# A four-layer attention kernel: the MLP in blocks of 512 pixels and two rounds, and a reordered top

## The chip, the cores and the metric

The kernel runs on one core of one Trainium2 chip, in one launch. The metric is the device time of an execution in microseconds, the median of the runs shown. A second execution under the hardware profiler gave the profile and the trace; TensorE's granted clock in it is 1.00 of full speed.

## What is computed

The input is `x`, two images of 512 channels and 32 x 32 pixels, all in float32. Four layers follow each other:

- Layer 0, deformable attention and an MLP. Queries come from a grouped 1x1 convolution. A strided depthwise convolution of the queries gives 64 offsets for each of the 8 groups of each image, at which keys and values are sampled. A small network of 2 inputs, 128 and 128 inner units and 1 output is evaluated for every pair of a pixel and a sample: `relu(relu(pos @ w1 + b1) @ w2 + b2) @ w3 + b3`. It is added to the attention logits. After softmax, values and output projection come `x = x + out` and the MLP:

```
xn2 = bn(x, bn2_g, bn2_b)
h1 = gelu(mlp_w1 @ xn2 + mlp_b1)        # 512 -> 2048 channels
x = x + mlp_w2 @ h1 + mlp_b2            # 2048 -> 512 channels
```

- Layers 1 and 2, group norm and self attention over the 1024 pixels, with 8 heads and with 1 head, and a projection with a bias.
- Layer 3, attention with 64 query and key channels and a factor `gamma`.

## The kernel before, in words

**Order of the work.** Each engine runs its instructions in the order in which the Python program emits them: `in_order` (line 61) ties each instruction to the one before it on its engine. Semaphores between engines come from what the tiles are written and read by. So a statement that moves in the program moves in the queue of every engine that it uses. DMAs are issued from the queues of SyncE, ScalarE and POOL, among the other instructions of that queue.

**The top (lines 205 to 900).** ScalarE's queue issues the loads of the query weights, of the first quarter of image 0 and of the weights of layer 2. `transposed(j, k)` transposes four 128x128 pieces of row block `k` of `qkv2` (`j`: q, k or v) on TensorE, and ScalarE copies them to SBUF. With these, `fold` multiplies layer 2's weights into each other. `bias_weights` sorts the inner units of the small network, `offsets(0)` computes the first offsets on VectorE, and `small_fold` computes two bias vectors of layer 2. The second of these is a row of 512 numbers: four matmuls `pb` (line 880), each of 32 weight columns that repeat one column of the value bias, write four groups of 32 partitions; ScalarE copies the result to `o_row`, and four DMAs spread it over the partitions. `bias_row` (line 1795) does the same for layer 1 as one of the chores between matmul groups.

**The pair loop (lines 901 to 993).** 256 steps. `first` (line 615) makes two tiles of the first inner layer on VectorE with one custom instruction, `second` (line 632) multiplies them by `cpb_w2`, four matmuls of 32 columns side by side, and ScalarE takes the relu. Sums of the results go through VectorE and accumulating DMAs. The results lie in two rings, `h2p` and `h2j`, which were slices of the tile `bridge` (8 x 4 KB per partition), and the tiles of `first` in `ring`.

**The end of the attention.** `finish_last` (line 733) runs the last softmax and projection, and between its steps forms what the MLP needs: `normed_rights` computes the normed pixels of the first block on POOL and their sums on VectorE, `left_sums` the sums of the columns of `mlp_w1`.

**The MLP (lines 1283 to 1395).** Both products use the seven-product form of a two by two block product (Strassen-Winograd): `lefts` and `rights` form sums of the four blocks of the weights and of the pixels, `products` runs seven products, and `combined` adds them up on VectorE. The pixels come in blocks of `BLK` = 256, of which each half of `PX` = 128 is one side of the block product, so matmuls have 128 moving columns. For each of 8 blocks there are 8 chunks `c` of the first product; each yields 128 lower and 128 upper inner units (2048 in all). ScalarE copies product 1 from PSUM (`first_of`), VectorE combines, ScalarE applies Gelu (`activated`), VectorE forms the sums of the right side for the second product (`form_right2`). The second product has two output chunks of 8 k-steps and ends in `added`, which adds bias and residual and stores the result to DRAM (`x_d`) for a fallback path. In PSUM the seven products of a chunk lay in two banks of 512 float32, four in each.

Between these, group norm of layer 1 advances in steps (`norm`), whose last four write the normed image `hc` with ScalarE; the sums of `mlp_w2` are formed in block 0 (`later`); in the last block the weights `qkv1` are loaded into the place of `mlp_w1`.

## Time and profile before

| | us |
|---|---|
| median of 3 runs | 3326.72 (3326.65 to 3328.97) |
| the profiled execution | 3326.56 |
| its span | 3324.8 |
| TensorE busy | 3311.0 |
| VectorE busy | 2643.8 |
| ScalarE busy | 1809.0 |
| POOL busy | 672.8 |
| first matmul of the pair loop (L632) | at 53.82 |
| first matmul of the MLP (pma) | at 1999.67 |
| first matmul of layer 1 (pm) | at 2402.69 |

The span is the time from the first to the last instruction of the program. Of each group of instructions the profile gives line, engine, operation, the tiles that it writes and reads, the shape and the count, then busy time and mean duration, then idle time before it and what ended that. L632 is line 632 of the kernel. PE is TensorE's matmuls, PEld its weight loads, which run beside them, DVE is VectorE, ACT ScalarE, SP SyncE; a q behind a name is the engine's queue, which issues DMAs. A float32 matmul call leaves two matmul records and two weight loads in the trace. The ends of matmuls are modelled and overlap the next one's start, so rates are taken from start to start.

### The profile page before, as it was taken

What the parts mean: (1) busy time and instruction counts of PE and PEld (TensorE: products, weight loads), DVE (VectorE), ACT (ScalarE), POOL (GpSimd) and SP (SyncE); (2) the same over time, 40 slices, a digit from 0 to 9 for tenths busy, and PEclk for the clock granted to TensorE, in tenths of its full rate; (3) what the DMA queues carried; (4) which work ended last, traced back from release to release, by engine and by line L of the source; (5) the groups of instructions that cost most, each with busy time, mean ns of one, the idle gap of its engine ahead of it and who ended that gap; (6) DMA issues with size and microseconds to landing.
All of it is one profiled execution on the core that took longest, in us unless ns stands there. A gap on an engine that the chain in (4) does not pass through costs nothing.

```text
span 3324.8 us, 60957 instructions
## 1 busy us (share of the span) xinstructions
PE 3311.0 (100%) x24805; PEld 1599.6 (48%) x24805; DVE 2643.8 (80%) x3027; ACT 1809.0 (54%) x2771; POOL 672.8 (20%) x804
## 2 busy tenths in 40 slices
PE   9999999999999999999999999999999999999999
PEld 4333333333333333333333339999953443687777
DVE  7999999999998799999999976455446466665656
ACT  4866877877876677877877642122126245122221
POOL 1333333333333233333333310000000000000000
PEclk9999999999999999999999999999999999999999
DMA  5787787787787577787787741000100100000111
GB/s 177 164 168 151 159 167 158 160 166 152 160 167 159 107 160 155 159 170 158 163 164 155 160 116 58 14 8 14 52 0 14 26 32 17 7 7 4 29 33 37
DMA packets 143121, 342.87 MB, mean 103 GB/s; under 512 B 37104, under 2 KB 52592, under 8 KB 142064
## 3 DMA queue, kind: packets, MB, share of 16 engines
q0 software_dynamic: 68112, 230.21, 37.1%
q1 hardware_dynamic: 71472, 102.12, 10.1%
q10 hardware_dynamic: 3248, 6.56, 0.5%
q8 instruction: 197, 3.23, 0.4%
q14 instruction: 92, 0.75, 0.1%
HBM read 71.46 MB, written 10.83 MB: 25 GB/s over the span
## 4 chain that ended last, share of the span: by engine, by line
PE 97%; issue 1%; ACT 1%; DVE 1%; POOL 0%; ACTq 0%; DVEq 0%; POOLq 0%
PE z L632 53%; PE pw L1479 6%; PE pma L135 6%; PE pmb L135 5%; PE pmv L1479 4%; PE score L1660 4%; PE pv L1672 3%; PE pm L1479 3%; PE score L1479 3%; PE pmt L1479 1%; PE ppr L1479 1%; PE pp L721 1%; PE sim L661 1%; PE pf L135 1%; PE pma L1382 1%
## 5 line engine op out<-in xcount | busy, mean ns | idle before, releaser
L632 PE MATMUL z<-wa,cpb_w 128*32 128x512 f32 x10880 | 1193.1, 593 | 0.5
L641 ACT ACTIVATE h<-z,b2h 128x1024 f32<-128x1024 f32 x768 | 851.2, 1113 | 327.7 <-PE z L632 316.9
L615 DVE CUSTOM_DVE_ANT_1 wa<-tab,pairs 128x2048 f32<-128x2048 f32 x340 | 779.3, 2293 | 2.7 <-PE z L632 2.4
L632 PEld LDWEIGHTS z<-wa,cpb_w 128*32 128x32 f32 x10880 | 346.1, 110 | 806.0 <-issue 713.5
L632 PE MATMUL z<-h,cpb_w 128*32 128x512 f32 x5504 | 609.4, 593 | 0.3 <-ACT h L641 0.2
L615 DVE CUSTOM_DVE_ANT_1 h<-tab,pairs 128x2048 f32<-128x2048 f32 x172 | 394.4, 2294 | 1.2 <-PE z L632 1.0
L632 PEld LDWEIGHTS z<-h,cpb_w 128*32 128x32 f32 x5504 | 175.4, 110 | 409.5 <-issue 360.1
L646 DVE SCALAR_TENSOR_TENSOR h<-h,turn,h 128x1024 f32<-128x1024 f32 x256 | 329.4, 1287 | 5.5 <-ACT h L641 5.5
L641 ACT ACTIVATE bridge<-z,b2h 128x1024 f32<-128x1024 f32 x162 | 180.6, 1115 | 118.2 <-PE z L632 118.2
L966 POOL DMA_DIRECT2D bridge<-bridge x150 | 127.5, 850 | 532.7 <-DMA bridge<-h 502.3
L646 DVE SCALAR_TENSOR_TENSOR bridge<-bridge,turn,h 128x1024 f32<-128x1024 f32 x162 | 208.1, 1285 | 3.0 <-ACT bridge L641 2.9
L974 POOL DMA_DIRECT2D bridge<-h x160 | 150.3, 939 | 287.3 <-DVE h L646 166.2
L1322 ACT COPY p<-pma 128x128 f32<-128x128 f32 x80 | 21.2, 266 | 335.7 <-PE pma L135 335.7
L1314 DVE TENSOR_TENSOR upper<-pma,p 128x256 f32<-128x256 f32 x80 | 33.8, 422 | 178.9 <-ACT p L1322 178.8
L1661 ACT ACTIVATE p<-score 128x512 f32<-128x512 f32 x256 | 129.7, 628 | 79.8 <-PE score L1660 79.4
L966 POOL DMA_DIRECT2D h2j<-h2j x90 | 76.2, 846 | 312.3 <-DMA h2j<-h 296.7
L1693 DVE TENSOR_TENSOR acc<-acc,p 128x1024 f32<-128x1024 f32 x96 | 111.4, 1219 | 28.4 <-ACT p L1661 28.4
L641 ACT ACTIVATE h2j<-z,b2h 128x1024 f32<-128x1024 f32 x94 | 104.9, 1116 | 42.7 <-PE z L632 42.7
L646 DVE SCALAR_TENSOR_TENSOR h2j<-h2j,turn,h 128x1024 f32<-128x1024 f32 x94 | 121.1, 1288 | 0.2
L1660 PE MATMUL score<-q,k 64*128 64x512 f32 x512 | 119.6, 604 | 0.0
L1672 PE MATMUL pv<-p,vT 128*64 128x512 f32 x512 | 116.5, 598 | 0.0
L979 POOL DMA_DIRECT2D bridge<-bridge x90 | 110.4, 1226 | 1.2 <-DMA bridge<-bridge 0.9
(468 smaller groups left out, 4363.2 us busy)
## 6 DMA issues: line engine op xcount, KB each, us to landing
bridge<-h POOLq DMA_DIRECT2D x160, 512.0 KB, 5.1
h2j<-h POOLq DMA_DIRECT2D x93, 512.0 KB, 5.5
bridge<-bridge POOLq DMA_DIRECT2D x159, 256.0 KB, 3.6
tab<-slog_d SPq DMA_DIRECT2D x128, 256.0 KB, 5.0
h2j<-h2j POOLq DMA_DIRECT2D x90, 256.0 KB, 3.3
bridge<-bridge POOLq DMA_DIRECT2D x150, 128.0 KB, 5.4
bridge<-bridge SPq DMA_DIRECT2D x90, 128.0 KB, 3.7
bridge<-h2j SPq DMA_DIRECT2D x90, 128.0 KB, 3.6
```

What stands on the lines that cost most here:

```text
L135: nc.tensor.matmul(pm, w, m, start=(k == 0), stop=(k == len(pairs) - 1))
L615: nc.vector._custom_dve(TENSOR_ADD_SAT, out=h1, in0=tx.unsqueeze(1).to_broadcast([P, H, 2, W]), in1=ty.unsqueeze(3).to_broadcast([P, H, 2, ...
L632: nc.tensor.matmul(z[point * 32 : point * 32 + 32, n], cpb_w2[:, lo : lo + 32], h1s[point][:, half * 16 : half * 16 + 16, :], start=True, ...
L641: nc.scalar.activation(h2, z, AF.Relu, bias=b2h[:, part : part + 1])
L646: nc.vector.scalar_tensor_tensor(h2, h2, turn[:, part // 2 : part // 2 + 1], parts.pop(part + 1), ALU.mult, ALU.add)
L966: nc.gpsimd.dma_start(out=own[0:P:2], in_=own[1:P:2], accum_op=ALU.add)
L974: nc.gpsimd.dma_start(out=joins[i - 1], in_=other, accum_op=ALU.add)
L1479: nc.tensor.matmul(out, stationary(l, k), moving(r, k), start=start and k == 0, stop=k == nk - 1, skip_group_check=not start,)
L1660: nc.tensor.matmul(sc, ks[m][r, s * P : (s + 1) * P], qs[m][r, n], start=True, stop=True)
L1661: nc.scalar.activation(p[:, part], sc, AF.Exp, scale=64 ** -0.5)
L1672: nc.tensor.matmul(pv[half][part * 64 : part * 64 + 64], vt[s % 4][:, lo : lo + 64], lps[s, half][:, part, :], start=(s == 0), stop=(s == 7),)
L1693: nc.vector.tensor_add(acc[half], acc[half], ps[s, half])
```

## The change

In the MLP, `BLK` becomes 512, so there are 4 blocks and matmuls of 256 moving columns. Each block is worked in two rounds (`rnd`): a round does the first product for half of the chunks (`RC` = 4) and then the part of the second product that sums over these inner units. The first round of a block adds its result and the bias to `x`, the second adds its result and stores. The seven products of a chunk lie in four banks (`slots`), are issued in the order 1, 6, 7, 5, 4, 2, 3, and `combined` takes them in six operations. The second product starts with three k-steps of product 1 for both output chunks, then product 2, then the last k-step of product 1. The buffers of the normed pixels and the rings of the pair loop move: `hc` is one tile for the whole program, `bridge` is split in `bridge_b` and `h1_0`, and the first tile of `ring` becomes the place of the normed pixels. In `finish_last` the normed pixels are computed at the start and their sums ahead of the maxima; the last projection's result is read half by ScalarE and half by VectorE. In the top, the transposes of row block 1 come earlier and four loads on ScalarE's queue later. The bias rows' matmuls read the weights in their own order, and the copy from PSUM does the reordering.

```diff
-    BLK = 256
+    BLK = 512
...
     def normed_rights(blk):
-        xn = bridge[:, 6, :].rearrange("p (k n) -> p k n", k=CC)
+        xn = h1_0.rearrange("p (k n) -> p k n", k=CC)
...
-        form(slice(0, CC // 2))
-        return right
+        return right, lambda: form(slice(0, CC // 2))
...
-        h2p = cycle([bridge[:, k, :] for k in range(6)])
-        h2j = cycle([bridge[:, 6, :], bridge[:, 7, :], *(...)])
+        h2p = cycle([*(hc[:, k, :] for k in range(4)), *(bridge_b[:, k, :] for k in range(2))])
+        h2j = cycle([bridge_b[:, 2, :], bridge_b[:, 3, :], *(...)])
...
-        ring = [one.tile([P, 2 * HW], F32, name=f"h1{k}") for k in range(2)]
+        ring = [h1_0, one.tile([P, 2 * HW], F32, name="h1_1")]
...
         def finish_last(...):
             table(AF.Exp)
+            right_sums()
...
             project_out(pps[0], b, 0, [2])
+            form_right.pop()()
...
-            right_sums()
...
                     project_out(pps[m], b, m, range(NPAIR) if m >= 2 else [pr], [half])
-                    add_out(b, m, n, pps[m])
+                    if half and m == CC - 1:
+                        mine, its = [slice(HALF + k * HALF // 2, HALF + (k + 1) * HALF // 2) for k in range(2)]
+                        rest = h2q.tile([P, HALF // 2], F32, name="rest", tag="h2")
+                        nc.scalar.activation(rest, pps[m][:, its], AF.Identity, bias=col("out_b", m))
+                        add_out(b, m, mine, pps[m])
+                        nc.vector.tensor_add(xs[b][:, m, its], xs[b][:, m, its], rest)
+                    else:
+                        add_out(b, m, n, pps[m])
...
         for j in range(3):
             transposed(j, 0)
-        load_groups("kw")
-        vb2 = ...; nc.scalar.dma_start(out=vb2, ...)
-        nc.scalar.dma_start(out=xs[0][:, 1:, :], ...)
         for pr in range(1, NPAIR):
             query_bias(pr)
         nc.vector.tensor_copy(qb[:, 1:], pqb[:, 1:])
+        transposed(0, 1)
         row = ...
         bias_steps = bias_weights()
+        transposed(1, 1)
         next(bias_steps)
         key_steps = key_weights()
+        transposed(2, 1)
+        load_groups("kw")
+        vb2 = ...; nc.scalar.dma_start(out=vb2, ...)
+        nc.scalar.dma_start(out=xs[0][:, 1:, :], ...)
         advance(steps, 4)
         advance(bias_steps)
-        for j in range(3):
-            transposed(j, 1)
...
-                    proj2[:, k, :].rearrange("p (m q) -> p q m", m=CC),
+                    proj2[:, k, :],
...
-            nc.scalar.copy(o_row, pb)
+            nc.scalar.copy(o_row.rearrange("p (q m) -> p m q", m=CC), pb.rearrange("p (m q) -> p m q", m=CC))
...
+            def slots():
+                some = [bank(f"pm{i}").rearrange("p (j n) -> p j n", j=2) for i in "abcd"]
+                a, b, c, d = some
+                return some, {6: a[:, 0], 1: a[:, 1], 4: b[:, 0], 5: b[:, 1], 7: c[:, 0], 3: d[:, 0], 2: d[:, 1]}
+
+            def product(at, i, left, right, k0, cols, ks, nk):
                 l, r = left[i - 1], right[i - 1]
+                for k in ks:
+                    nc.tensor.matmul(at[i], l[:, k0 + k, cols], r[:, k, :], start=(k == 0), stop=(k == nk - 1))
+
+            def combined(some, at, lower):
                 upper = two.tile([P, 2, PX], F32, name="upper")
                 u = two.tile([P, 2, PX], F32, name="u")
+                p1 = two.tile([P, PX], F32, name="p1")
+                nc.scalar.copy(p1, at[1])
+                nc.vector.tensor_tensor(upper[:, 1], at[6], p1, ALU.add)
+                nc.vector.tensor_tensor(u[:, 1], at[7], upper[:, 1], ALU.add)
+                nc.vector.tensor_tensor(u[:, 0], at[5], upper[:, 1], ALU.add)
+                nc.vector.tensor_tensor(lower, some[1], u[:, 1].unsqueeze(1).to_broadcast([P, 2, PX]), ALU.add)
+                nc.vector.tensor_tensor(upper[:, 0], at[2], p1, ALU.add)
+                nc.vector.tensor_tensor(upper[:, 1], at[3], u[:, 0], ALU.add)
...
-            def added(blk, m, src):
+            def added(blk, m, src, last):
...
-                nc.vector.scalar_tensor_tensor(x, src, col("mlp_b2", m), x, ALU.add, ALU.add)
+                if not last:
+                    nc.vector.scalar_tensor_tensor(x, src, col("mlp_b2", m), x, ALU.add, ALU.add)
+                    return
+                nc.vector.tensor_add(x, x, src)
                 nc.sync.dma_start(out=x_d[b, m, :, at : at + BLK], in_=x)
...
-            for blk in range(NBLK):
+            RC = MC // 2
+            for blk, rnd in [(blk, rnd) for blk in range(NBLK) for rnd in range(2)]:
+                last = (blk, rnd) == (NBLK - 1, 1)
+                lo = rnd * RC
...
-                for c in range(MC + 1):
+                for c in range(RC + 1):
+                    if c < RC:
+                        some, at = slots()
+                        for i in (1, 6, 7, 5, 4, 2, 3):
+                            product(at, i, left1, right1, 0, slice((lo + c) * P, (lo + c + 1) * P), range(CC // 2), CC // 2)
                     if c:
                         activated(c - 1, upper)
+                    if c < RC:
+                        upper = combined(some, at, hid[:, RC + c, :].rearrange("p (j n) -> p j n", j=2))
                     if c:
                         form_right2(slice(c - 1, c))
-                    if blk == 0 and 4 <= c < MC - 1:
+                    if blk == rnd == 0 and c == 2:
                         advance(later[0])
-                    if b == 1 and c % 2:
+                    if blk == 2 and c in (1, 2, 3) or blk == 3 and c in (1, 3):
                         advance(norm)
...
+                if last:
...
+                    drain(norm)
+                elif rnd:
+                    right1, form = normed_rights(blk + 1)
+                    form()
...
+                both = [slots() for c in range(2)]
+                for i, ks in ((1, range(RC - 1)), (2, range(RC)), (1, range(RC - 1, RC))):
                     for c in range(2):
+                        product(both[c][1], i, left2, right2, lo, cols[c], ks, RC)
                 for c in range(2):
+                    for i in (6, 7, 5, 4, 3):
+                        product(both[c][1], i, left2, right2, lo, cols[c], range(RC), RC)
...
-        drain(norm)
...
-                    proj1[k // 2][:, k % 2, :].rearrange("p (m q) -> p q m", m=CC),
+                    proj1[k // 2][:, k % 2, :],
...
-            nc.scalar.copy(row, pb)
+            nc.scalar.copy(row.rearrange("p (q m) -> p m q", m=CC), pb.rearrange("p (m q) -> p m q", m=CC))
```

## The prediction

> **What bounds the kernel now.** I read the page first, then the waits of TensorE, then its timeline around the two places that the change touches, and last the rows of the other engines in the MLP.
>
> ```profile
> span 3324.8 us, 60957 instructions
> ...
> PE 3311.0 (100%) x24805; PEld 1599.6 (48%) x24805; DVE 2643.8 (80%) x3027; ACT 1809.0 (54%) x2771; POOL 672.8 (20%) x804
> ...
> PE 97%; issue 1%; ACT 1%; DVE 1%; POOL 0%; ACTq 0%; DVEq 0%; POOLq 0%
> ```
>
> TensorE is busy for the whole span and holds 97% of the chain that ended last. So only two things save time: TensorE work that becomes shorter, and waits of TensorE that go. The list of its waits (engine, line, waited for: us in total, times, longest) shows how little the second can give:
>
> ```profile
> PE pma L1382 <- ACT hid L1347: 0.9, 1, 0.9
> PE pma L135 <- POOL ones L1336: 0.9, 1, 0.9
> ```
>
> The first is inside the MLP's first block, the second at its start; with some 1.9 us in pieces of 0.2 to 0.5 us between 10 and 20 us, and 0.5 us at L778, that is all outside the ends. The MLP runs from 1999.67 (first pma) to 2402.69 (first matmul of the next layer): 403.0 us. The timeline of TensorE there, and in a stage that multiplies 256 columns (start, us, engine, line, operation, names, shapes, count):
>
> ```profile
> 2081.60 1.95 PE L135 MATMUL pma<-hidt,w2s 128*128 128x128 f32 x16
> ...
> 2099.46 1.95 PE L135 MATMUL pma<-hid,w2s 128*128 128x128 f32 x16
> ```
> ```profile
> 3015.69 3.62 PE L1479 MATMUL pmv<-wa,hc 128*128 128x256 f32 x16
> 3019.14 2.75 PE L1479 MATMUL pmv<-wa,h2t 128*128 128x256 f32 x12
> 3021.73 2.75 PE L1479 MATMUL pmv<-wa,hc 128*128 128x256 f32 x12
> 3024.32 1.03 PE L1479 MATMUL score<-t,hc 128*128 128x256 f32 x4
> ```
>
> Start to start, 160 matmuls of 128 columns take 17.86 us, 0.1116 us each; 40 of 256 columns take 8.63 us, 0.2158 us each, not 0.2232. (The trace's "mean ns" of 275 and 379 overlap and are no rate.)
>
> **Part 1: blocks of 512 pixels in two rounds.** Each matmul call leaves two records. Before: 8 blocks x (8 inner chunks x 7 products x 2 k-steps + 2 output chunks x 7 x 8) = 1792 calls, 3584 records of 128 columns. After: 4 blocks x 2 rounds x (4 x 7 x 2 + 2 x 7 x 4) = 896 calls, 1792 records of 256 columns. From the rates: 3584 x 0.1116 = 400.0; 1792 x 0.2158 = 386.7; 13.3 us less. The 403.0 us also hold the 0.9 us wait and 2.1 us of small hand-overs (L1382 takes 3.71 us for 32 records, 0.14 over the rate, once per block). I leave 0.5 us for those after, so 387.2 against 403.0: **-15.8 us**.
>
> Here a rule speaks against the change. The Trainium skill, "TensorE: Matmul & The Clock Gate", section "Wait — 56ns, not 53.3ns?", says that a warm matmul costs N ÷ 2.4 GHz and a fixed 2.5 ns or so, whatever N. Halving the count would then save 1792 x 2.5 ns = 4.5 us. The rows say otherwise: two streams of 128 columns cost 2 x 111.6 - 215.8 = 7.4 ns more than one of 256, three times the rule, and the weight loads fill the window of block 2 (50.14 of 50.20 us on PEld) where they filled 10.64 of 12.30 us at 256 columns. I take the rows; 4.5 us is kept as a rival.
>
> **Does another engine take over?** Per inner chunk TensorE needs 28 records x 0.2158 = 6.04 us. VectorE's rows:
>
> ```profile
> L1315 DVE TENSOR_TENSOR u<-pmb,upper 128x256 f32<-128x256 f32 x78 | 33.1, 424 | 2.7
> ...
> L1532 DVE SCALAR_TENSOR_TENSOR k<-pm,pc,u 128x512 f32<-128x512 f32 x8 | 6.0, 748 | 0.1
> ```
>
> The new combination is five operations of 256 columns and one of 512, 5 x 0.42 + 0.75 = 2.9 us; the four sums of the right side are 256 wide, 4 x 0.42 = 1.7 us: 4.6 us of 6.04, about what it was (before, 24.95 us in a block of 50.2 plus waits). A bn_stats step of the group norm (two of 0.67 us and a little) makes it some 6.0 in three chunks of block 2; there it just fits, and four chunks ahead of the next hand-over absorb a remainder. ScalarE has a copy (0.37) and two Gelus of 512 (0.63 each by the Exp of that width at L1661): 1.6 us.
>
> Hand-over to the second product (T = end of a round's first product): TensorE now does 3 k-steps of product 1 for both output chunks (12 records, 2.6 us), product 2 (16 records, to T+6.0), the last k-step of product 1, then from T+6.9 the products that need sums. Product 2 needs the lower Gelu: its operand is done some 0.5 us before T, since products 4 and 5 are no longer last. The upper Gelu ends near T+1.8; VectorE finishes its eight pending sums near T+4.2. All are earlier than their use by over 2 us. In the first round seven of the eight sums of w2 (1.22 us each) are queued behind these, to T+12.8: the first that is needed, the second sum of chunk 0, is ready at T+5.5 for T+6.9, the last for T+15.5 and later. What waits behind them on VectorE is the combination of output chunk 0, which has 8 banks and another 8 us of matmuls as cover. POOL's four operations, now 512 wide (0.54 us for 256 without VectorE beside it, 1.2 with it: 4.5 to 9 us), and the four sums that wait for them (0.7 us each) end by T+12 of the 24 us. The four norm activations (1.23 us each) move from the last block to behind the last Gelu on ScalarE, because they write where the left sums lie: T+1.8 to T+6.9, needed at T+24; the copy of p1 queued behind them comes due at T+8.6. Loading qkv1 (10 us in the trace) keeps its 24 us. Half as many x_d stores of twice the size go on SP; nobody waits for them.
>
> **Part 2: the bias rows.** The same four matmuls read their moving rows at a stride of 128 elements before, in their own order after.
>
> ```profile
> 44.57 2.26 PE L880 MATMUL pb<-wa,vb 128*32 128x512 f32 x8
> 46.75 7.13 PE L135 MATMUL pf<-wa,bridge 128*128 128x512 f32 x16
> ```
> ```profile
> 1941.83 13.92 PE L632 MATMUL z<-wa,cpb_w 128*32 128x512 f32 x128
> ...
> 1955.56 7.05 PE L632 MATMUL z<-h,cpb_w 128*32 128x512 f32 x64
> ```
>
> Eight strided records hold TensorE for 2.18 us. The z matmuls have the same shape (32 columns of weights, four column groups side by side) and read in order: 13.73 us for 128, 0.107 each, so 8 take 0.86 us. Saved 1.3 us, and the same at L1799 (2601.45 to 2603.64): **-2.6 us**. Bounds: 0, if the stride is not the cause, and 2.8. The stride goes to ScalarE's copy (0.585 us). The skill's "SBUF — State Buffer", section "Door 1: The DMA port swizzle", says that accesses which each cross to a new line of 16 bytes pay, and the copy now writes at 16-byte steps; even at double its cost nothing waits: ScalarE is idle for 6.5 us after it. Starting the pair loop 1 us earlier is harmless: the smallest distance from a finished h1 pair (L615) to its first matmul is 3.6 us, near 131 us.
>
> **Part 3: the top.** Three transposes (q, k, v of row block 1) move ahead of the four loads on ScalarE's queue, to fill TensorE's gaps.
>
> ```profile
> 11.47 0.60 ACTq L238 DMA_DIRECT2D bridge<-in_kw  x1
> ...
> 13.44 0.91 ACTq L828 DMA_DIRECT2D x<-in_x  x1
> 14.38 0.27 ACT L311 COPY sort<-prow 128x128 f32<-128x128 f32 x1 [2.23 <-DVE sums L432]
> ```
>
> The four issues hold ScalarE's queue for 2.9 us (11.47 to 14.35), where it had little to do. After, they start behind the third new copy, near 14.6, and end near 17.5; the copy of pw2t and the six remaining copies (0.49 us each) queue behind. The fifth of these ends near 20.4, and the first fold matmul starts near 20.5 instead of 20.17: the gaps are filled but the issues are moved into ScalarE's busy stretch. **+0.3 us**; between -1.0 (if the issues overlap the copies) and +1.2. The loads land 3 us later; kw (18.8 before) is used at 28.7, x at 71.
>
> **Part 4: the end of the attention.** The last projection's read of PSUM (0.75 us on VectorE, behind which TensorE waits 0.9) is halved, but VectorE's half waits for ScalarE's in the built program: about 0.4 + 0.5 us in a row, **+0.2** (-0.3 if side by side). The right sums of block 0 (four of 0.7 us) run from about 1971.1, when the sim matmuls have read their places, to 1973.9, ahead of the maxima, which start at 1974.26: they fit by 0.3 us; if not, up to +0.5 at L778.
>
> Sum: -15.8 - 2.6 + 0.3 + 0.2 = -17.9. The profiled execution took 3326.56 (span 3324.8 and 1.8 around it), so 3308.7; the median of the runs is 0.2 above it: **3308.8 us**.
>
> **Rivals.** (a) *A hand-over wait in each round*, for a late Gelu or sum: for it, 0.9 us was lost so in the first block; against it, the 2 us of cover above. Eight rounds x 1 us: 3316.8. (b) *The rule's fixed cost*: 4.5 us instead of 13.3, so 3317.6. (c) *More than I count*: the top gains 1 us instead of losing 0.3, no hand-over cost, halves of the last read side by side: 3308.8 - 1.3 - 0.5 - 0.5 = 3306.5. (d) *Slower*: VectorE sets the pace of the first product. From 6.04 + 17.9/32 = 6.6 us per inner chunk on the 32 chunks eat the gain; at 7.0 us they cost 32 x 0.96 = 30.7 us: 3339.5. For it: it is the engine with the most work there, and POOL shares its time in parts; against it, the sum of 4.6 us from rows of the same operations.
>
> **How the numbers follow.** Forecast 0.68 (its own range 3307 to 3311), (a) 0.12, (b) 0.04, (c) 0.12, (d) 0.04. Leaving out (b), (d), the far half of (a) and a little at the bottom gives 3306 to 3316. A measurement of this kernel tells about 0.2% (6.7 us) from no change; below 3320.1 are the forecast, (c), (a) and nearly all of (b): faster 0.94, same 0.02, slower 0.04.
>
> **What would show it.** 1792 MLP records of 128x256 at 0.216 us start to start; the MLP at 387 us; no wait at its hand-overs; the pb matmuls at 0.9 us twice; the first fold at 20.3 to 20.7 us. A row of equal TensorE gaps at the rounds, or VectorE busy through them, makes me wrong.

## The result, and the profile after

| | before | after |
|---|---|---|
| median (lowest to highest of 5 runs), us | 3326.72 (3326.51 to 3328.97) | 3308.71 (3307.89 to 3309.28) |
| the profiled execution, us | 3326.56 | 3309.28 |
| its span, us | 3324.8 | 3307.2 |
| first fold matmul (pf) | 20.17 | 19.70 |
| first matmul of the pair loop | 53.82 | 52.16 |
| first matmul of the MLP | 1999.67 | 1999.04 |
| first matmul of layer 1 | 2402.69 | 2386.33 |

The ratio is 0.9945, with a 95% interval from 0.9934 to 0.9955. The forecast was 3308.8.

The page of the kernel after:

```profile
span 3307.2 us, 56997 instructions
...
PE 3294.7 (100%) x23013; PEld 1540.6 (47%) x23013; DVE 2647.1 (80%) x2852; ACT 1801.6 (54%) x2676; POOL 666.2 (20%) x788
...
PE 98%; ACT 1%; DVE 1%; issue 0%; ACTq 0%; POOL 0%; POOLq 0%; DVEq 0%
```

TensorE still holds the chain. It has 24805 - 23013 = 1792 records fewer, exactly the MLP's halving. Its list of waits:

```profile
PE pma L1314 <- POOL ones L1344: 1.2, 1, 1.2
PE tw L801 <- ACT sort L343: 1.0, 1, 1.0
```

(These are its longest, but for one of 2.3 us ahead of TensorE's first matmul that stands in both lists.) The wait inside the MLP (`pma` for `hid`, 0.9 us) is gone, and no hand-over of the eight rounds is in the list. The wait at the MLP's start grew from 0.9 to 1.2, and one of 1.0 us in the top is new: two of the small parts, to which the experiments come back. The timeline of TensorE at the end of a round (start, us, engine, line, operation, names, shapes, count):

```profile
2205.45 1.03 PE L1314 MATMUL pma<-bridge_b,hc 128*128 128x256 f32 x4
...
2215.81 1.03 PE L1314 MATMUL pmd<-h,bridge_b 128*128 128x256 f32 x4
2216.67 2.75 PE L1314 MATMUL pma<-hid,wb 128*128 128x256 f32 x12
2219.26 3.62 PE L1314 MATMUL pmd<-hid,wb 128*128 128x256 f32 x16
2222.71 1.03 PE L1314 MATMUL pma<-hid,wb 128*128 128x256 f32 x4
2223.58 0.59 PE L1314 MATMUL pma<-hidt,w2s 128*128 128x256 f32 x2
```

From 2205.45 to 2222.71 lie 80 records, 0.2158 us each. The first product ends at T = 2216.67 and the second follows without a gap. ScalarE and VectorE at the same place:

```profile
2216.61 0.72 ACT L1357 ACTIVATE hid<-hid,pc 128x512 f32<-128x512 f32 x1 [3.63 <-DVE hid L1325]
2217.66 0.72 ACT L1360 ACTIVATE hid<-upper,pc 128x512 f32<-128x512 f32 x1 [0.33 <-DVE upper L1327]
```
```profile
2219.01 1.28 DVE L1238 BATCH_NORM_STATS2 st<-x 128x6 f32<-128x512 f32 x2
...
2221.53 0.42 DVE L176 TENSOR_TENSOR hidt<-hid,hidt 128x256 f32<-128x256 f32 x1
```

The lower Gelu ends at T+0.7 (needed at T+2.6), the upper one at T+1.7 (needed at T+6.0), the last sum at T+5.3 (needed at T+6.9), and this is a round that also has the group norm's statistics on VectorE.

Where the 17.60 us of the span went, from the starts of the named matmuls in the two traces:

| stage | before | after | difference | forecast |
|---|---|---|---|---|
| to the first fold matmul | 20.17 | 19.70 | -0.47 | +0.3 |
| bias row of layer 2 (first pb to next matmul) | 2.19 | 1.00 | -1.19 | -1.3 |
| pair loop, to the start of its last step | 1901.75 | 1902.47 | +0.72 | 0 |
| from there to the first pma | 44.11 | 44.41 | +0.30 | +0.2 |
| MLP | 403.02 | 387.29 | -15.73 | -15.8 |
| bias row of layer 1 | 2.19 | 0.99 | -1.20 | -1.3 |
| after it | 721.13 | 721.09 | -0.04 | 0 |

The other stages are equal to 0.02 us.

### The profile page after: what moved, and what is told of

Read it like the earlier page. It is cut to its first block, busy times and chain, and to the rows that moved or that the text cites. A ratio compares the mean times of both kernels' runs of the same rounds, so it can differ in the third digit from the quotient of the medians.

```text
span 3307.2 us, 56997 instructions
## 1 busy us (share of the span) xinstructions
PE 3294.7 (100%) x23013; PEld 1540.6 (47%) x23013; DVE 2647.1 (80%) x2852; ACT 1801.6 (54%) x2676; POOL 666.2 (20%) x788
## 4 chain that ended last, share of the span: by engine, by line
PE 98%; ACT 1%; DVE 1%; issue 0%; ACTq 0%; POOL 0%; POOLq 0%; DVEq 0%
PE z L632 53%; PE pw L1488 6%; PE pmv L1488 4%; PE score L1669 4%; PE pv L1681 3%; PE pma L1314 3%; PE pmd L1314 3%; PE pmb L1314 3%; PE pm L1488 3%; PE score L1488 3%; PE pmc L1314 2%; PE pp L721 2%; PE pmt L1488 1%; PE ppr L1488 1%; PE sim L661 1%; PE pf L135 1%
## 5 line engine op out<-in xcount | busy, mean ns | idle before, releaser
L976 POOL DMA_DIRECT2D bridge_b<-bridge_b x110 | 93.3, 848 | 379.0 <-DMA bridge_b<-h 354.0
L641 ACT ACTIVATE bridge_b<-z,b2h 128x1024 f32<-128x1024 f32 x116 | 129.3, 1115 | 67.5 <-PE z L632 66.3
L646 DVE SCALAR_TENSOR_TENSOR bridge_b<-bridge_b,turn,h 128x1024 f32<-128x1024 f32 x116 | 148.3, 1279 | 1.0 <-ACT bridge_b L641 0.9
L984 POOL DMA_DIRECT2D bridge_b<-h x115 | 111.6, 970 | 121.0 <-DVE h L646 82.8
L1321 ACT COPY p<-pma 128x256 f32<-128x256 f32 x48 | 17.9, 372 | 183.9 <-PE pma L1314 175.3
L984 POOL DMA_DIRECT2D h2j<-h x93 | 93.2, 1002 | 47.1 <-DVE h L646 35.4
L1488 PE MATMUL pmv<-wa,hc 128*128 128x256 f32 x384 | 89.5, 380 | 0.0
```

Source lines behind the costliest of these rows:

```text
L641: nc.scalar.activation(h2, z, AF.Relu, bias=b2h[:, part : part + 1])
L646: nc.vector.scalar_tensor_tensor(h2, h2, turn[:, part // 2 : part // 2 + 1], parts.pop(part + 1), ALU.mult, ALU.add)
L976: nc.gpsimd.dma_start(out=own[0:P:2], in_=own[1:P:2], accum_op=ALU.add)
L984: nc.gpsimd.dma_start(out=joins[i - 1], in_=other, accum_op=ALU.add)
L1488: nc.tensor.matmul(out, stationary(l, k), moving(r, k), start=start and k == 0, stop=k == nk - 1, skip_group_check=not start,)
```

## Experiments

The theory is that of the prediction: the MLP gains because 128-column records are held up by their weight loads, the bias rows because of the stride, and the rest is small. Nothing of the computation is left out in any of these kernels. Where a kernel ran only once, what is said of it rests on the stage in its trace rather than on its time.

**The bias rows alone, in the kernel before.**

```diff
-                    proj2[:, k, :].rearrange("p (m q) -> p q m", m=CC),
+                    proj2[:, k, :],
...
-            nc.scalar.copy(o_row, pb)
+            nc.scalar.copy(o_row.rearrange("p (q m) -> p m q", m=CC), pb.rearrange("p (m q) -> p m q", m=CC))
```

> The kernel before with the bias rows alone in their own order. Theory (the stride costs TensorE time): each row's eight records hold TensorE for 0.99 us instead of 2.19, as in the changed kernel, so 2.4 us less in all, 3324.3 us, and no other stage moves. Rival (what is saved at the top is lost again, because the pair loop then starts closer behind VectorE): the first pb is shorter but the loop ends where it did, 1.2 us less.

Measured: 3324.20 us (12 runs) against 3326.82, 2.6 us less; ratio 0.9993 (0.9984 to 1.0001). The interval of the ratio reaches 1, so the time alone doesn't show the gain, but in its trace both rows take 0.99 us and all other stages are those of before to 0.2 us, save that the first fold starts 0.06 us earlier.

**The MLP and the end of the attention alone.** The kernel after, with the top and the bias rows' matmuls of before.

```diff
-                    proj2[:, k, :],
+                    proj2[:, k, :].rearrange("p (m q) -> p q m", m=CC),
...
-        transposed(0, 1)
...
+        for j in range(3):
+            transposed(j, 1)
```

> The changed kernel with the top and the bias rows as before: the MLP, the moved buffers and the end of the attention alone. Theory: the MLP takes 387.3 us instead of 403.0, the end of the attention 0.3 more, so 15.4 us less than before: 3311.3 us. Rival (the moved buffers or the new order cost or save elsewhere): a difference from 15.4 of over 1 us that sits outside the MLP.

Measured: 3312.00 us (3310.95 to 3312.88), ratio 0.9956 (0.9939 to 0.9973). The MLP takes 387.30 us, as in the full change. The two kernels' gains, 2.6 and 14.8, add up to 17.4 of the full change's 18.0. What is left, 0.6, is no more than the reordered top and the spread of the runs account for, so nothing shows that the parts act on each other.

**The top undone.** The kernel after with the order of before in the top.

```diff
+        load_groups("kw")
+        vb2 = ...; nc.scalar.dma_start(out=vb2, ...)
+        nc.scalar.dma_start(out=xs[0][:, 1:, :], ...)
         for pr in range(1, NPAIR):
...
-        transposed(0, 1)
...
-        transposed(1, 1)
...
-        transposed(2, 1)
-        load_groups("kw")
...
+        for j in range(3):
+            transposed(j, 1)
```

> The changed kernel with the top in its old order. The first fold matmul came at 19.70 us in the changed kernel and 20.17 before. Theory A (the new order gained it): back to about 20.2, 0.5 us longer. Theory B (most of it is the arrival of the first loads, 0.3 us earlier in that execution): about 19.9, 0.2 us longer. My prediction's reckoning, that the new order loses 0.3, gives 19.4.

Measured: 3308.92 us (3308.37 to 3309.35), ratio 0.9946 (0.993 to 0.9963): the same time as the full change. Its first fold starts at 19.69, as early as in the kernel after, but in its execution the first loads also came earlier (the first matmul on them, `pq`, at 7.03 us against 7.30). From the first transpose to the first fold the old order takes 10.74 (before), 10.85, 10.85 and 10.82 us in the four traces that have it. The new order takes 10.36 (after), 10.25 to 10.61 in five more kernels below that change nothing in the top, and 11.37 in a sixth. So the new order mostly gains some 0.1 to 0.6 us there. The arrival of the first loads, which moves `pq` between 7.03 and 7.86 us in these executions, is larger than that, and in the time the two orders can't be told apart.

**Twice as many records in the MLP, with the rest unchanged.** The calls of 256 columns are cut in two of 128 each, so only the width differs; the short k-steps of the hand-over stay at 256.

```diff
-                for k in ks:
-                    nc.tensor.matmul(at[i], l[:, k0 + k, cols], r[:, k, :], start=(k == 0), stop=(k == nk - 1))
+                cuts = [slice(0, PX)] if len(ks) < nk else [slice(0, 128), slice(128, PX)]
+                for n in cuts:
+                    for k in ks:
+                        nc.tensor.matmul(
+                            at[i][:, n], l[:, k0 + k, cols], r[:, k, n], start=(k == 0), stop=(k == nk - 1)
+                        )
```

> The changed kernel with every MLP matmul of 256 columns cut in two of 128, each with its own weight load, but for product 1 of the second product (128 of the 1792 records). All else stays. Theory (a pair of 128-column records costs 7.4 ns more than one of 256): 1664 x 7.4 ns = 12.3 us longer, 3321.0 us, and the weight loads fill the window again. Rival (a fixed 2.5 ns for each matmul whatever its width): 4.2 us longer. Rival (the gain came from the rounds and the order, not from the width): no change.

Measured: 3321.62 us (3320.86 to 3322.34, 20 runs), ratio to before 0.9984 (0.9978 to 0.9991). The MLP takes 399.77 us, 12.48 more than the kernel after, for 1664 further records: 7.5 ns each. The forecast's rate gave 7.4, the rule's fixed cost 2.5. Blocks, rounds, buffers and order are those of the new kernel, so the width alone is most of what the MLP gained. Of the other 3.25 us, the 128 records left uncut are worth 0.9; the wait of 0.9 us in the first block and the small hand-overs of before (0.14 us in each of 8 blocks), which are gone, account for most of the rest.

**Uneven halves.** A fixed cost per record does not care where the cut is; a floor under each record does. The cut at 160 makes records of 160 and 96 columns, as many as the cut at 128.

```diff
-                cuts = [slice(0, PX)] if len(ks) < nk else [slice(0, 128), slice(128, PX)]
+                cuts = [slice(0, PX)] if len(ks) < nk else [slice(0, 160), slice(160, PX)]
```

> As the run with halves of 128, but cut in 160 and 96 columns. It tells apart what the 7.4 ns are. Theory L (weight loads set a floor of 111.6 ns for a record, however few columns follow): 160 columns take 135.8 ns, 96 columns take 111.6, so 31.6 ns more for each of 1664 records, 52.6 us longer than the changed kernel. Theory F (a fixed cost of some 5 ns for each narrow matmul): 12 us longer at most. The rule's fixed 2.5 ns: 4.2 us longer.

Measured: 3362.86 us (one run). The MLP takes 439.96, 52.67 more than in the kernel after. Its timeline of TensorE; a group's shape is that of its first record, and each group holds as many of 96 columns as of 160:

```profile
2094.05 2.15 PE L1316 MATMUL pmb<-hidt,w2s 128*128 128x160 f32 x16
2096.03 2.15 PE L1316 MATMUL pmb<-hidt,wb 128*128 128x160 f32 x16
```

16 records take 1.98 us, so a pair takes 0.247, where one record of 256 columns takes 0.216: 31.6 ns more, by 1664. Over the MLP the median from start to start is 136 ns after a record of 160 columns and 111 to 112 after one of 96, the same as after one of 128. At the slope between the 256- and the 160-column records, (216 - 136) / 96 = 0.83 ns a column, 96 columns would take 83 ns. The first record of each run of 96-column records does take 83, but the first of 160 columns behind the run then takes 165 instead of 136, and all the others of 96 take 111 to 112. So a sequence of records that each have their own weights of 128 columns does not keep a pace below 112 ns here, however short its streams.

That the weight loads set this floor is borne out by three things. First, their busy time: they fill a block of the kernel before, and leave room in a round of the kernel after (windows of one block and of one round; the busy times are PE, PEld, DVE, ACT and POOL, then the granted clock, the DMA share and GB/s):

```profile
2051.10:2101.30 50.20, 50.20 (x451) 50.14 (x450) 24.95 (x80) 9.18 (x26) 2.54 (x4) 1.00 0.04 12
```
```profile
2047.50:2095.90 48.40, 48.40 (x226) 42.61 (x225) 26.84 (x60) 8.01 (x14) 3.05 (x4) 1.00 0.03 12
```

Second and third, two other places in the kernel after, with TensorE's rows first and then the rows of the weight loads (their mean time in ns stands behind the comma):

```profile
23.24 0.95 PE L348 MATMUL pparts<-pc,sort 128*128 128x2 f32 x8
555.97 1.09 PE L684 MATMUL pt<-cst,simb 128*128 128x128 f32 x8
```
```profile
L348 PEld LDWEIGHTS pparts<-pc,sort 128*128 128x128 f32 x8 | 1.1, 192 | 0.5 <-issue 0.5
L684 PEld LDWEIGHTS pt<-cst,simb 128*128 128x128 f32 x8 | 0.9, 140 | 0.8 <-ACT h L641 0.8
```

Records with only 2 moving columns follow each other at 112 ns from start to start, after a first one at 28; their loads are like the MLP's, which the trace shows at 190 ns. Transposes, whose records have 128 moving columns but whose loads the trace shows at 140 ns instead, keep 109 ns, which is what the slope gives for 128 columns (136 - 32 x 0.83). So the 112 ns go with the load and not with the columns.

The rule of the Trainium skill ("TensorE: Matmul & The Clock Gate", "Wait — 56ns, not 53.3ns?"), N ÷ 2.4 GHz and some 2.5 ns, would make 256 columns take 109 ns (an estimate from its figures). They take 216: these float32 records cost 0.83 ns a column, twice what N ÷ 2.4 GHz gives. With 0.83 put into it, its fixed 2.5 ns fits the wide records, 215.8 and 135.8 ns against 216 and 136 in the runs. For 128 and 96 columns it then gives 109.2 and 82.5, where the runs show 112 for both. What it leaves out is the floor, and the floor is what this kernel stood on.

**How much VectorE may have to do.** Three or six needless additions of 256 columns behind each step of the first product's loop. The loop has five steps in a round, so they are 120 and 240 in all, not the 96 that the first expectation counts.

```diff
                     form_right2(slice(c - 1, c))
+                    for _ in range(3):
+                        nc.vector.tensor_tensor(idle, cst[:, :PX], cst[:, :PX], ALU.add)
```

> The changed kernel with three needless additions of 128x256 behind the four sums of each inner chunk on VectorE (96 in all, 0.46 us each, 1.4 us for each chunk). Theory (VectorE has 1.4 us or more to spare in each 6.04 us): no change, within 0.7 us. Rival d of the prediction, if VectorE were nearly the pace: up to 32 x 1.4 = 44 us longer.

Measured: 3308.95 us (one run), MLP 388.38, 1.09 more. That is 0.4 us more than the expectation allowed. All of it is in the first round, where the sums of `w2` run too; the other seven rounds are those of the kernel after to 0.01 us.

```profile
PE pma L1314 <- DVE w2s L161: 0.8, 1, 0.8
```

The prediction gave that first sum 1.4 us of slack (T+5.5 for T+6.9). In the kernel after it ends at T+5.0, so the slack was 1.9; the additions ahead of it move its end to T+7.8, and the loss is 1.09.

> The same with six, 2.8 us for each inner chunk. By rival d's reckoning (4.6 + 2.8 = 7.4 us for a chunk against 6.04) 32 x 1.3 = 43 us longer. Theory (the lag gathers over the four chunks of a round only, the banks cover it, and it shows at the hand-over alone, where product 6 waits for the last sums by 1 to 2 us): 8 to 16 us longer, all of it as one TensorE wait for VectorE at the start of each round's second product.

Measured: 3326.83 us (one run), MLP 405.32, 18.03 more. The waits of TensorE in the MLP, and windows of it, with columns as above:

```profile
PE pma L1314 <- DVE w2s L161: 5.5, 1, 5.5
PE pma L1314 <- DVE hidt L174: 3.3, 2, 1.7
PE pg L1244 <- DVE mean L1251: 2.6, 1, 2.6
...
PE pmd L1314 <- ACT hid L1358: 0.8, 1, 0.8
```
```profile
2035.50:2041.00 5.50, 5.42 (x13) 4.36 (x14) 5.47 (x6) 0.37 (x1) 0.00 (x0) 0.50 0.00 0
2041.00:2060.00 19.00, 19.00 (x89) 16.69 (x88) 10.24 (x21) 0.74 (x2) 0.00 (x0) 0.99 0.00 1
```

Between the starts of the products, five of the sixteen half rounds are longer than in the kernel after, by 8.59, 2.99, 2.85, 1.68 and 1.92 us; the sum, 18.0, is the whole difference. They are the second product of round 1 (sums of `w2`), of round 5, the first and second product of round 6 (group norm's statistics and `mean`), and the second product of round 8. Not all of it is waiting. Behind the wait of 5.5 us, 12 records start 427 ns apart instead of 216, at a granted clock of 0.50 (the first window above), and 7 do so behind the wait of 2.6 us. That is some 4 us (19 x 0.211) of the 18.0, and nearly all of the loss in the second product of round 6. The expectation, 8 to 16 us in equal waits at every hand-over, missed both the size and the places. In the other eleven half rounds, six additions in each chunk (2.75 us) cost nothing: VectorE may fall behind within four chunks, because the second product gives it time to catch up. Rival (d)'s arithmetic, in which every microsecond above 6.6 per chunk is paid 32 times, is wrong in its shape; VectorE is nearer to being late in the first round and in the group norm than in the steady pace.

**The hand-over without its reordering.** The last k-step of product 1 is put back with the first three, so the upper Gelu is needed at once.

```diff
-                for i, ks in ((1, range(RC - 1)), (2, range(RC)), (1, range(RC - 1, RC))):
+                for i, ks in ((1, range(RC)), (2, range(RC))):
```

> The changed kernel with the second product beginning with all four k-steps of product 1, so that the last upper Gelu is due 1.3 us after the first product's end instead of 6.0. The Gelu ends 1.7 us after it in the changed kernel. Theory: 0.4 to 0.6 us of wait for ScalarE in each of 8 rounds, 3 to 5 us longer. Rival (the order makes no difference): no change.

Measured: 3312.38 us (one run), MLP 391.44, 4.15 more.

```profile
PE pma L1314 <- ACT hid L1360: 1.8, 6, 0.3
```

At each of the eight hand-overs two records that take 2 x 0.216 us elsewhere take 0.69 + 0.32 (six times) or 0.46 + 0.32 (twice). So a wait of 0.31 us costs 0.57 where it is read from start to start. Of the 0.26 more, 0.16 is a matter of reading: the profile counts the wait from the modelled end of the record before it, 0.38 us after that record's start, while the next would have started after 0.216. The other 0.10 is lost because the record after the wait takes 0.32. No weight load started during the wait (the loads stand still for 0.71 us), and the load for the following record starts only 0.11 us after the waiting record. This is rival (a)'s mechanism at half its price. In the kernel after, the order of the k-steps is what keeps it from coming.

**The last read of the attention in one piece.**

```diff
-                    if half and m == CC - 1:
-                        ...
-                        nc.vector.tensor_add(xs[b][:, m, its], xs[b][:, m, its], rest)
-                    else:
-                        add_out(b, m, n, pps[m])
+                    add_out(b, m, n, pps[m])
```

> The changed kernel with the last projection's result read whole by VectorE, as before. Theory (the two halves are read one after the other): TensorE's wait ahead of the MLP goes from 1.18 to 0.89 us, 0.3 us shorter. Rival (the wait has another cause, as the buffers that moved): it stays at 1.18.

Measured: 3308.46 us (one run). TensorE's wait ahead of the MLP is 0.89 us again, where the kernel after has 1.18. The reads in the kernel after, and then in this one:

```profile
1997.94 0.47 ACT L790 ACTIVATE rest<-pp,pc 128x256 f32<-128x256 f32 x1 [16.63 <-DVE bridge_b L161]
1998.45 0.48 DVE L731 SCALAR_TENSOR_TENSOR x<-pp,pc,x 128x256 f32<-128x256 f32 x1 [0.55 <-ACT rest L790]
```
```profile
1997.59 0.75 DVE L731 SCALAR_TENSOR_TENSOR x<-pp,pc,x 128x512 f32<-128x512 f32 x1
```

Halved, the read is 0.47 + 0.48 in a row, because VectorE waits for ScalarE; whole, it is 0.75. This part of the change is a loss of 0.29 us.

**The four loads on SyncE's queue.** If the loads' issues hold up ScalarE in the top, a queue that is free could take them.

```diff
-        load_groups("kw")
+        load_groups("kw", nc.sync)
...
-            nc.scalar.dma_start(out=vb2, ...)
+            nc.sync.dma_start(out=vb2, ...)
...
-        nc.scalar.dma_start(out=xs[0][:, 1:, :], ...)
+        nc.sync.dma_start(out=xs[0][:, 1:, :], ...)
```

> The changed kernel with the four loads that moved on ScalarE's queue issued from SyncE's queue instead. Theory (the issues hold ScalarE's queue, and TensorE's 1.0 us wait at 16.3 us is for the pw2t copy behind them): the wait goes, the first fold matmul comes 0.8 to 1.0 us earlier, at 18.8, and the pair loop with it. Rival (the wait is for the third transposes' rows, or the copies of 0.49 us each set the pace from there): 0.3 us or less.

Measured: 3314.56 us (one run), 5.9 more than the kernel after. The waits of TensorE:

```profile
PE tw L801 <- DMA wa<-in_qkv_w: 5.3, 3, 2.2
```

A window behind the last of these waits, with columns as above (the granted clock is 0.50):

```profile
20.50:22.00 1.50, 1.40 (x7) 1.43 (x8) 1.39 (x6) 0.28 (x1) 0.00 (x0) 0.50 0.85 314
```

SyncE had nothing ahead of the loads, so they went out between 2.1 and 5.0 us, beside the loads of `qkv2_w`, which the transposes need. Those landed at 11.43, 14.75 and 20.46 us instead of 9.21, 11.09 and 14.87, and the first fold started at 25.18. Behind the last wait, of 2.24 us, 14 transposes started 213 ns apart instead of 109 while the clock was at 0.50; that is some 1.5 us of the loss. The place in ScalarE's queue is also what holds the loads back. The same with the read in one piece:

> The changed kernel with both: the loads on SyncE's queue and the last result read whole. Theory: 1.2 us shorter than the changed kernel, 3307.5 us, and 19.2 us shorter than before. If either of the two single runs shows nothing, its part is missing here.

Measured: 3313.12 us (3312.77 to 3314.37), ratio to before 0.9959 (0.9945 to 0.9972). The wait ahead of the MLP is 0.89, as it should be, and the first fold starts at 24.38: not a better kernel.

**The loads on ScalarE's queue again, behind the last transposes' copies, and the read in one piece.**

```diff
         transposed(2, 1)
-        load_groups("kw")
-        vb2 = ...; nc.scalar.dma_start(out=vb2, ...)
-        nc.scalar.dma_start(out=xs[0][:, 1:, :], ...)
...
         for k in range(2, CC):
             for j in range(3):
                 transposed(j, k)
+        load_groups("kw")
+        vb2 = ...; nc.scalar.dma_start(out=vb2, ...)
+        nc.scalar.dma_start(out=xs[0][:, 1:, :], ...)
```

> The changed kernel with the last read of the attention in one piece, and with the four loads of Part 3 (kw twice, vb, x) issued by ScalarE again, but behind its last transposes' copies instead of ahead of the copy that TensorE waits for. Nothing of the computation is left out. Theory: on ScalarE's queue the loads go out only when the copies ahead of them are done (about 20 us), so the three loads of qkv2_w land as in the changed kernel (the last at about 14.9 us, not at 20.5 as when SyncE issued the four early), TensorE's wait of 0.99 us ahead of the bias transposes goes, and the first fold starts 0.7 to 1.0 us earlier, at 18.7 to 19.0 us if the first loads arrive as in the changed kernel's trace; kw lands by 25 us, ahead of its transposes at 28. With the 0.29 us of the single read the kernel takes 0.7 to 1.3 us less than the changed one: 3307.4 to 3308.0 us. Rival: the wait only passes to the next link (the copies of the transposes, or the bias rows' weights), and the first fold starts within 0.3 us of before: 3308.2 to 3308.6 us; or kw now comes late at 28 us, and TensorE waits for it there: 3309 us or more.

Measured: 3307.29 us (3306.70 to 3307.54), against 3326.64 of the kernel before beside it; ratio 0.9940 (0.9927 to 0.9954). That is a little under the expected 3307.4 to 3308.0. It is 1.4 us less than the kernel after, and the two sets of five runs do not overlap; the intervals of the ratios do. ScalarE's timeline in the top of the kernel after:

```profile
13.65 0.59 ACT L802 COPY hc<-tw 128x512 f32<-128x512 f32 x1 [0.77 <-PE tw L801]
14.26 0.27 ACT L311 COPY sort<-prow 128x128 f32<-128x128 f32 x1
14.32 0.60 ACTq L238 DMA_DIRECT2D bridge_b<-in_kw  x1
...
16.29 0.52 ACTq L851 DMA_DIRECT2D x<-in_x  x1
16.85 0.37 ACT L343 ACTIVATE sort<-pw2t,few 128x128 f32<-128x128 f32 x1 [1.84 <-PE tw L801]
...
19.49 0.64 ACT L802 COPY bridge_b<-tw 128x512 f32<-128x512 f32 x1
```

And of this kernel:

```profile
13.53 0.59 ACT L795 COPY hc<-tw 128x512 f32<-128x512 f32 x1 [0.77 <-PE tw L794]
14.14 0.27 ACT L311 COPY sort<-prow 128x128 f32<-128x128 f32 x1
...
15.03 0.37 ACT L343 ACTIVATE sort<-pw2t,few 128x128 f32<-128x128 f32 x1
...
18.06 0.63 ACT L795 COPY bridge_b<-tw 128x512 f32<-128x512 f32 x1
18.62 0.63 ACTq L238 DMA_DIRECT2D bridge_b<-in_kw  x1
...
19.94 1.46 ACTq L909 DMA_DIRECT2D x<-in_x  x1
```

The copy of `pw2t` no longer stands behind four issues, TensorE's wait of 1.0 us is gone from its list, and the first fold starts at 18.25 instead of 19.70 (0.37 of it because the first transpose came earlier; from there to the first fold it takes 9.28 us instead of 10.36). `kw` lands at 22.2 us and is still early for its transposes, at 26.8.

## Why the prediction was right, and where it was not

**Part 1** held in its working: 0.2158 us per record, 387.29 us against 387.2. One of its sums does not close: 0.14 us in each of 8 blocks is 1.1, not the 2.1 us that it puts to small hand-overs. In the trace of before the rest is mostly the cost of the one wait beyond its 0.9 us (0.3) and four small matmuls of the group norm (0.4). That it was the width, and not the regrouping, is shown by the cut at 128. The choice of the row over the rule, which decided between -15.8 and some -7 us, is confirmed by both cuts, and the uneven one says why: a floor, not a fee per record. The prediction weighed only the rule's fixed part; that its N ÷ 2.4 GHz is half of what these float32 records take was not noticed, and the rates from the rows made it harmless. Of the times at the hand-over, the upper Gelu was put at T+1.8 and came at T+1.7. The lower Gelu was put 0.5 us before T and came at T+0.3 to T+1.0, by round. The sums were put at T+4.2; they came at T+3.9 and T+4.3 in the first two rounds, and at T+5.3 in a round with group norm statistics, which that sum had left out. The cover was wide enough for all three. The additions show that the thinnest place was the one named, the first sum of `w2` in round one.

**Part 2** was right in its cause, a little large in its size. The rows after:

```profile
44.10 1.06 PE L890 MATMUL pb<-wa,vb 128*32 128x512 f32 x8
45.09 7.13 PE L135 MATMUL pf<-wa,bridge_b 128*128 128x512 f32 x16
```
```profile
45.23 1.09 ACT L898 COPY o_row<-pb 128x512 f32<-128x512 f32 x1
```

Eight records take 1.00 us rather than 0.86. From start to start the first four take 0.45, near the 0.43 of four in the middle of the pair loop, and the last four 0.54; the last four ahead of a full-width matmul take 0.54 in the pair loop too. The rate of 128 in a row has no such end in it. The gain is 2 x 1.2, not 2 x 1.3. The copy's price went from 0.585 to 1.09 us (at layer 1 from 0.59 to 1.10), close to the double that the prediction allowed, and nobody waited for it. That agrees with the direction of the skill's rule on 16-byte lines ("SBUF — State Buffer", "Door 1: The DMA port swizzle"), which gives no figure for such a copy.

**Part 3** is the step that failed, by 0.8 us: forecast +0.3, measured -0.47. The sum had the issues begin at 14.6 and end at 17.5, and the first fold at 20.5. They began at 14.32 beside a copy and ended at 16.81, since the last issue, 0.91 us before, took 0.52; the rest followed as forecast, to 19.70. The sign was taken from two terms that move between executions by as much as the sum. The wait that the step foresaw (the copy of `pw2t` behind the issues) is there: the last experiment takes it away, and from the first transpose to the first fold it takes 1.1 us less.

**Part 4** held: 0.47 + 0.48 us in a row, +0.30 against +0.2.

**What no part had** is 0.72 us in the pair loop. It arises at one place, near 903 us, and the rest of the loop is equal to the kernel with the top undone, to 0.03 us. TensorE there in the kernel after, and then in that kernel:

```profile
901.34 2.16 PE L661 MATMUL sim<-hc,w 128*32 128x512 f32 x15
903.06 0.60 PE L632 MATMUL z<-wa,cpb_w 128*32 128x512 f32 x3
903.34 0.59 PE L661 MATMUL sim<-hc,w 128*32 128x512 f32 x1
```
```profile
901.33 1.90 PE L661 MATMUL sim<-hc,w 128*32 128x512 f32 x16
903.05 5.33 PE L632 MATMUL z<-wa,cpb_w 128*32 128x512 f32 x48
```

One of the sixteen `sim` matmuls, which run four side by side in groups of 32 columns, started only after three of the next matmuls, and by the end of the stretch 0.7 us were lost. A loss at this same place stands in three other executions (0.33, 0.39 and, in the last experiment, 0.65 us), and in none of eight others with the same loop. So it is not of the change. What sets it off was not found. By luck it covered Part 3's error: -17.60 measured and -17.9 forecast agree better than the parts do.

Of the rivals, (a) and (b) are excluded by the traces and by the cut kernels, (d) by the six additions. (c) was right about the top in part, and wrong about the halves, which this program reads one after the other.

## What to carry to other kernels

Read a matmul's rate from start to start at two widths before trusting either a mean or a fixed cost. If the rate is a floor set by the weight loads, wider moving operands pay until the load fits under the stream (the time in which a record's moving columns pass), and an uneven cut, with one part under the floor, costs far more than an even one. Where a DMA issue stands in a compute engine's queue, ask both what waits behind it and what it is held behind: moved later on the same queue, the four loads here gained over a microsecond, moved to a free queue they cost more than five, partly because a wait of TensorE halved its clock. When a slack is claimed, load the engine until it breaks: where it breaks first (here the first round and the group norm) is not where the average says.

## What was not expected of the hardware

- In a sequence of float32 records that each load weights of 128 columns, one takes 112 ns for 2, 96 or 128 moving columns alike; at 160 and 256 columns it takes 136 and 216.
- After TensorE had waited 5.46 us, 12 of its next records of 256 columns started 427 ns apart, at a granted clock of 0.50, and then 216 again: the wait cost another 2.5 us (12 x 0.211). After a wait of 2.61 us the same happened to 7 records, though the first few behind it still started 216 ns apart, and with the loads on SyncE's queue 14 transposes ran at half rate after waits of 2.24 and 2.47 us. After waits of 1.68 us and less it happened to none. The skill's "TensorE: Matmul & The Clock Gate", "Part 1: The HAM clock gate (the "warmup" mystery)", has the half rate and an idle window of some 3.4 us; the 2.24 to 2.61 us here are less than that.
- One of sixteen matmuls that run side by side in column groups started late, behind three of the next matmuls, in the kernel after. At this place four of twelve executions of the same loop lost 0.33 to 0.72 us, the others nothing.
- A wait of TensorE costs more than the profile's figure for it: 0.31 us cost 0.57 at the hand-over, 0.10 of it because the next record took 0.32 us instead of 0.216.
